# Deferring the lower-half transposed columns of the first image into layer 0, and taking the low part of h from SBUF

## The chip, the cores and the metric

The kernel runs on one core of a Trainium2 chip. The metric is the device time of one execution in microseconds (us). Three runs of the kernel before gave 3059.95, 3065.07 and 3065.65 us; their median is 3065.07 us.

## What is computed

The input `x` has 4 images of 16 channels and 256x256 pixels. Two layers follow each other, each adding to its input a function of the group-normalised input (8 groups of 2 channels):

```
def _L0_conv_ref(x, conv_w, conv_b):                 # K = 5
    out = conv 3x3 of x, 16 -> 16*25 channels, + conv_b
    weights = softmax over the 25 logits of each channel
    return sum over the 5x5 neighbourhood of (x shifted) * weights
...
x = x + _L0_conv_ref(_gn(x), conv_w, conv_b)
x = x + _L1_conv_ref(_gn(x), ...)                    # 3x3, silu and cubic splines
```

The change concerns layer 0 and what prepares its input h = `_gn(x)`. The logits are matrix products that must be nearly exact in fp32: part of the contraction (channel rows of two of the three column shifts and most of the third) is done in fp32, and the rest in the faster fp32r format, for which h is split into a high part `hi` (h rounded to fp32r) and a low part `lo` = h - `hi`.

## The kernel before

**Prologue** (lines 404 to 589). Half-images of `x` (128 rows, 16 channels) are loaded one after the other, and VectorE (`bn_stats`), ScalarE (squares, line 543) and TensorE (line 546) gather the statistics of all four images. While it does this for images 1 to 3, the generator `normalize(0, ...)` is advanced between the statistics (lines 540, 541, 550), so that image 0, which is held in SBUF (`held`), is normalised beside it. The end of the prologue is a flag computed from all images (line 589), on which all engines branch.

**`normalize(b, ...)`** (lines 264 to 401) writes three DRAM scratch tensors of an image: `hs` (h by rows, for the 5x5 sums), and for each half h = 0, 1 of the image `hst[b][h]` (transposed columns of h in fp32) and `hsl[b][h]` (their `hi` and `lo` parts). It works by groups q of 4 channels (4 of them). `rows(q)` makes for each half two ScalarE activations into `hsp` (line 327) and two into `ht` (line 340); `hsp` is stored by `put_rows`. `columns(q, n, h)` (line 349; n = 0, 1) makes four TensorE transposes of `ht` into a PSUM tile `tp`, copies `tp` to the SBUF tiles `tt` (fp32) and `hi` (fp32r), 128x512 elements each, copies one edge column of four elements to the other half, and makes `lo` on VectorE:

```
nc.vector.tensor_sub(
    los[n][:, h, :, 1 : 1 + P], tp, his[n][:, h, :, 1 : 1 + P].bitcast(F32)
)
```

One input of that subtraction, `tp`, is in PSUM and one, `hi`, is in SBUF. After both halves of a pair (q, n), `border` copies the edge columns of `lo`, and `put_columns` issues six DMAs of 260 KB on SP's queue (three for each half). There are 16 steps `columns` to an image. Each is followed by empty steps, so that it takes six steps of the generator; `moves` is a list of actions that fall due some steps later. In the prologue `tt` is copied by VectorE, in layer 0 by ScalarE.

**Layer 0** (`layer0`, lines 620 to 883) runs over 64 strips: 4 images, 2 halves, 8 strips of 32 columns. A strip has 8 groups of 4 columns. For a group, TensorE makes the logits `lg` (three matmuls to a column: two passes of L833 for the fp32 part and one of L837 for the fp32r part), ScalarE takes their exponential into `e` (L856, twice to a group), GpSimd (POOL) multiplies `e` with the 5x5 neighbours `u` (L861, 128x1600 elements, both inputs in SBUF), and VectorE (DVE) sums products and weights (L700, a reduction of 128x3200 elements). There are four `e` tiles. Once to a strip three short VectorE operations divide (L720 to L722; one input of each is the PSUM tile `r`), and POOL subtracts the result from x (L728). The loads of a strip (`am` from `hst`, `an` from `hsl`, `u` from `hs`, `xc` from x) are issued on SP's queue, `am` and `an` two loads ahead.

The preparation of image b+1 runs in layer 0 of image b: after each group, `next(ahead)` (line 870) advances `normalize(b + 1, ...)` by one step. So in layer 0 every operation of `normalize` stands between those of two groups in its engine's queue. The order in the prologue is a scheduler's; in layer 0 `in_order` (line 591) makes it the order in which the code is written.

**Layer 1** (lines 886 to 1110) follows with VectorE, ScalarE and TensorE; POOL has only small operations in it.

Of the kernel before, what the change touches and what calls it, by code (L numbers as in the profile page):

```python
# [3 lines left out]

# [7 lines left out]
F32 = mybir.dt.float32  # L12
F32R = mybir.dt.float32r
AF = mybir.ActivationFunctionType
# [20 lines left out]
def conv_preact_kernel(  # L35
# [12 lines left out]
    nc = tc.nc  # L48
    B, C, H, W = x.shape
    G = 8  # L50
    GC = C // G
    P = 128
    NH = H // P
# [3 lines left out]
    PAD = K // 2  # L57
# [3 lines left out]
    SW = 32  # L61
    NST = W // SW
    SP = SW + 2 * PAD
# [4 lines left out]
    RP = P + 2  # L68
    CT = (W + 2) * RP
    QC = 4  # L70
    QW = W // (P // QC)
    QG = 4
# [8 lines left out]
    const = ctx.enter_context(tc.tile_pool(name="const", bufs=1))  # L81
# [42 lines left out]
    for r in range(RT):  # L124
        p = P // 2 + SROWS.index(r + 1) * C
# [118 lines left out]
    zpad = const.tile([P, QC, PAD], F32, name="zpad")  # L244
    nc.vector.memset(zpad, 0.0)

    def zeros(b, queue):

        for e in (0, HP - PAD):
            for r in range(PAD):  # L250
                yield partial(
                    queue.dma_start,
                    hs[b][:, e + r].rearrange("s c w -> c s w"),
                    zero[0:C, 0 : NST * SP].rearrange("c (s w) -> c s w", s=NST),
                )
        for h in range(NH):
            for w in (0, (W + 1) * RP):
                yield partial(queue.dma_start, hst[b][h][:, w : w + RP], zero[0:C, 0:RP])
                yield partial(
                    queue.dma_start,  # L260
                    hsl[b][h][:, :, w : w + RP].rearrange("c t r -> (c t) r"), zero[:, 0:RP],
                )

    def normalize(b, ptr, tiles, held=None, copier=None):

        prep, xps, tts, his, los = tiles
        copier = copier or nc.scalar.copy

        moves = [(20 + 4 * i, f) for i, f in enumerate(zeros(b, nc.sync))] if held is None else []

        def move():
            for f in [f for i, f in moves if i <= 0]:
                f()
            moves[:] = [(i - 1, f) for i, f in moves if i > 0]

        def load(q, h):
            if held is None and q < C // QC:
                nc.sync.dma_start(  # L280
                    xps[h][:, :, PAD : PAD + W],
                    x[b, q * QC : (q + 1) * QC, h * P : (h + 1) * P, :].rearrange(
                        "c p w -> p c w"),
                )

        def put_rows(q, h, hsp):
            r0 = PAD + h * P
            nc.sync.dma_start(
                hs[b][:, r0 : r0 + P, q * QC : (q + 1) * QC, :].rearrange(
                    "s r c w -> r s (c w)"),  # L290
                hsp.rearrange("p s c w -> p s (c w)"),
            )

        def put_columns(q, n):
            g0 = n * QG
            for h in range(NH):

                for to, ti, t in ((hst, 0, tts[n]), (hsl, 0, his[n]), (hsl, 1, los[n])):
                    d = to[b][h]
                    m = 2 if to is hsl else 1  # L300
                    t = t if t.dtype == F32 else t.bitcast(F32)
                    nc.sync.dma_start(
                        bass.AP(
                            tensor=d.tensor,
                            offset=d.offset + q * QC * m * CT + ti * CT + (1 + g0) * RP,
                            ap=[[QW * RP, W // QW], [m * CT, QC], [1, QG * RP]],
                        ),
                        t[:, h].rearrange("p g r -> p (g r)"),
                    )

        def border(t):
            nc.scalar.copy(t[:, 1, :, 0:1], t[:, 0, :, P : P + 1])
            nc.scalar.copy(t[:, 0, :, RP - 1 :], t[:, 1, :, 1:2])

        hts = {}

        def rows(q):
            for h in range(NH):
                xp = xps[h] if held is None else held[h][:, q * QC : (q + 1) * QC]
                hsp = prep.tile([P, NST, QC, SP], F32, name=f"hsp{b}_{q}_{h}", tag="hsp")  # L320
                ht = prep.tile([P, QW, W // QW, QC], F32, name=f"ht{b}_{q}_{h}", tag=f"ht{h}")
                hts[q, h] = ht
                for k in range(QC // GC):
                    g = q * (QC // GC) + k
                    kc = slice(k * GC, (k + 1) * GC)
                    how = dict(scale=nrm[b][:, 0, g : g + 1], bias=nrm[b][:, 1, g : g + 1])
                    nc.scalar.activation(
                        hsp[:, :, kc, :].rearrange("p s c w -> p c s w"),
                        bass.AP(
                            tensor=xp.tensor, offset=xp.offset + k * GC * (W + 2 * PAD),  # L330
                            ap=[xp.ap[0], [W + 2 * PAD, GC], [SW, NST], [1, SP]],
                        ),
                        AF.Identity, **how,
                    )
                    if k == QC // GC - 1:
                        nc.scalar.copy(hsp[:, 0, :, 0:PAD], zpad)
                        nc.scalar.copy(hsp[:, NST - 1, :, PAD + SW :], zpad)
                        moves.append((4, partial(put_rows, q, h, hsp)))
                    yield
                    nc.scalar.activation(  # L340
                        ht[:, :, :, kc].rearrange("p g w c -> p c w g"),
                        xp[:, kc, PAD : PAD + W].rearrange("p c (w g) -> p c w g", g=QW),
                        AF.Identity, **how,
                    )
                    if k == QC // GC - 1:
                        moves.append((4, partial(load, q + 1, h)))
                    yield

        def columns(q, n, h):

            tp = ptr.tile([P, QG, P], F32, name=f"tp{b}_{q}_{n}_{h}", tag="tp")

            def copy(t, to):

                to(t[:, h, :, 1 : 1 + P], tp)
                if h == 0:
                    to(t[:, 1, :, 0:1], tp[:, :, P - 1 :])
                else:
                    to(t[:, 0, :, RP - 1 :], tp[:, :, 0:1])

            for k in range(QG):
                nc.tensor.transpose(
                    tp[:, k, :], hts[q, h][:, n * QG + k].rearrange("p w c -> p (w c)"), ident
                )
            yield
            copy(tts[n], copier)
            copy(his[n], nc.scalar.copy)
            yield

            nc.vector.tensor_sub(  # L370
                los[n][:, h, :, 1 : 1 + P], tp, his[n][:, h, :, 1 : 1 + P].bitcast(F32)
            )
            if h == NH - 1:
                moves.append((5, partial(border, los[n])))
                moves.append((9, partial(put_columns, q, n)))
            yield
            yield
            yield
            yield

        for h in range(NH):
            load(0, h)
        yield
        for _ in rows(0):
            move()
            yield
        for q in range(C // QC):
            ahead = rows(q + 1) if q + 1 < C // QC else iter(())
            for n in range(QW // QG):
                for h in range(NH):  # L390
                    for k, _ in enumerate(columns(q, n, h)):
                        if k % 3 == 2:
                            next(ahead, None)
                        move()
                        yield
            for _ in ahead:
                move()
                yield
        while moves:
            move()  # L400
            yield


    with tc.tile_pool(name="prep0", bufs=2) as prep, tc.tile_pool(
# [121 lines left out]
        for b in range(B):  # L526
# [44 lines left out]
            if b == 1:  # L571
                prepare1()
            if b == 0:
                ahead = normalize(0, ptr0, tiles, held, nc.vector.tensor_copy)
                next(ahead)
        for _ in ahead:
            pass
# [42 lines left out]
    def layer0(shift):  # L620
# [4 lines left out]
        with tc.tile_pool(name=f"prep{arm}", bufs=2) as prep, tc.tile_pool(  # L625
# [172 lines left out]
            for n, (b, hf, s) in enumerate(strips):  # L798
                if (hf, s) == (0, 0):
                    for _ in ahead:  # L800
                        pass
                    ahead = normalize(b + 1, ptr, tiles) if b + 1 < B else iter(())
                    if b == B - 1:
                        bank = ptr.tile([P, QG, P], F32, name=f"ps{arm}", tag="tp")
                        first_scales = [scales(k, partial(lambda k: bank[:, k], k)) for k in range(2)]
                last = (hf, s) == (NH - 1, NST - 1)
                if last:
                    for _ in ahead:
                        pass
                u = us.pop(0)  # L810
                if s * SW % CX == 0:
# [350 lines left out]
```

## Time and profile before

| | |
|---|---|
| median of 3 runs | 3065.07 us |
| the profiled execution | 3061.86 us |
| its span, first to last instruction | 3059.8 us |
| mean granted TensorE clock | 0.971 |
| busy: TensorE, VectorE, ScalarE, POOL | 92%, 97%, 73%, 64% of the span |
| prologue, to the first layer 0 load | 0 to 120.4 us |
| layer 0, to the last reduction L700 | about 125 to 2047 us |
| layer 1 | about 2047 to 3060 us |

The profile is one execution of the program. A *group* of instructions shares line, engine, operation and tiles: its row has the busy time, the mean of one in ns, and then the idle time of the engine before them with what ended it. The *timeline* lists instructions in order of time with start and duration in us; equal ones that follow each other are merged (x7), and a bracket gives the idle time before and its releaser. A duration can contain a wait inside the instruction. *Busy by stretch* gives the busy time of each engine between two times. PE is TensorE, DVE VectorE, ACT ScalarE, SPq the queue of SyncE, which issues DMAs.

### The profile page before, as it was taken

The numbers are of one execution on the slowest core, as the hardware profiler recorded it, in microseconds if no ns is written. First come the engines' busy times: TensorE is split into PE (matmuls) and PEld (weight loads), VectorE is DVE, ScalarE is ACT, GpSimd is POOL, SyncE is SP. The second block draws the span as 40 slices with busy tenths as digits, with TensorE's granted clock in tenths as the row PEclk, the third lists the DMA queues.
The fourth block names the chain that finished last, engine by engine and source line by source line (L and its number), as shares of the span: only waits on it lengthen the run. The fifth ranks groups of instructions, "written<-read, shape, count | busy, mean of one in ns | idle before, by whom it ended". The sixth has DMA issues, their size and how long they took to land.

```text
span 3059.8 us, 39743 instructions
## 1 busy us (share of the span) xinstructions
PE 2802.6 (92%) x14248; PEld 1448.2 (47%) x14248; DVE 2959.0 (97%) x1587; ACT 2236.6 (73%) x2587; POOL 1947.6 (64%) x744
## 2 busy tenths in 40 slices
PE   4499999999999999999999999958999999999998
PEld 3366656656656666666666566632222222222222
DVE  7599999999999999999999999998999999999997
ACT  6466765676766566766646546559999999999996
POOL 4199999999999999999999999980100100000000
PEclk7699999999999999999999999978999999999999
DMA  8988977879878778978767667659999999999994
GB/s 273 290 223 221 258 205 209 222 189 257 234 209 240 196 202 225 248 216 220 212 174 200 164 173 194 161 131 198 201 192 195 198 194 189 198 194 202 190 197 91
DMA packets 350929, 626.29 MB, mean 205 GB/s; under 512 B 41330, under 2 KB 216676, under 8 KB 334852
## 3 DMA queue, kind: packets, MB, share of 16 engines
q1 hardware_dynamic: 318020, 605.29, 81.0%
q10 hardware_dynamic: 30960, 15.73, 1.8%
q0 software_dynamic: 1744, 2.64, 0.3%
q8 instruction: 117, 1.92, 0.3%
q14 instruction: 88, 0.72, 0.1%
HBM read 513.95 MB, written 104.24 MB: 202 GB/s over the span
## 4 chain that ended last, share of the span: by engine, by line
DVE 69%; issue 11%; PE 8%; DMA 3%; ACT 3%; POOL 2%; SPq 1%; DVEq 0%; ACTq 0%; POOLq 0%
DVE nd L700 44%; PE lg L833 6%; DVE ta L168 4%; DVE ta L167 4%; DVE tb L168 4%; DVE tb L167 4%; DVE tb L158 2%; PE lg L837 1%; DVE yo L1020 1%; POOL e L861 1%; DVE r L721 1%; DVE nd L720 1%; DVE lo L370 1%; DMA am<-hst 1%; DVE nd L722 1%
## 5 line engine op out<-in xcount | busy, mean ns | idle before, releaser
L861 POOL TENSOR_TENSOR e<-e,u 128x1600 f32<-128x1600 f32 x512 | 1788.4, 3539 | 49.0 <-ACT e L856 30.9
L833 PE MATMUL lg<-wm,am 128*128 128x400 f32 x4096 | 1734.8, 505 | 83.8 <-ACT e L856 53.0
L700 DVE TENSOR_REDUCE nd<-e 128x128 f32<-128x3200 f32 x512 | 1748.0, 3478 | 29.0 <-POOL e L861 28.9
L837 PE MATMUL lg<-wn,an 97*128 97x400 f32 x2048 | 1344.9, 657 | 17.3 <-DMA an<-hsl 17.3
L856 ACT ACTIVATE e<-lg 128x800 f32<-128x800 f32 x1024 | 818.2, 837 | 708.9 <-DVE nd L700 460.5
L833 PEld LDWEIGHTS lg<-wm,am 128*128 128x128 f32 x4096 | 760.9, 192 | 403.3 <-ACT e L856 98.2
L1037 PE MATMUL yp<-ring,wt 128*32 128x512 f32 x6144 | 745.9, 598 | 87.6 <-DVE ring L169 63.7
L837 PEld LDWEIGHTS lg<-wn,an 97*128 97x128 f32 x2048 | 388.3, 190 | 334.5 <-issue 23.6
L1037 PEld LDWEIGHTS yp<-ring,wt 128*32 128x32 f32 x6144 | 203.7, 109 | 621.7 <-issue 427.7
L954 POOL MEMSET sl<- 16x256 f32 x6 | 1.8, 306 | 402.7 <-ACT ta L163 299.8
L169 DVE SCALAR_TENSOR_TENSOR ring<-ta,ta 128x2048 f32<-128x2048 f32 (+1 forms) x64 | 147.9, 2310 | 2.5
L168 DVE TENSOR_TENSOR ta<-ta,ta 128x2048 f32<-128x2048 f32 (+1 forms) x64 | 147.5, 2305 | 2.8 <-ACT ta L166 2.8
L169 DVE SCALAR_TENSOR_TENSOR ring<-tb,tb 128x2048 f32<-128x2048 f32 x64 | 145.6, 2275 | 2.5
L748 ACT ACTIVATE z<-xc,nrm 128x256 f32<-128x256 f32 x240 | 144.2, 601 | 5.3 <-POOL xc L728 1.2
L168 DVE TENSOR_TENSOR tb<-tb,tb 128x2048 f32<-128x2048 f32 x64 | 145.4, 2271 | 0.0
L1047 PE MATMUL yp<-sl,ws 64*32 64x512 f32 (+1 forms) x1032 | 131.3, 602 | 0.0
L954 POOL MEMSET slc<- 16x256 f32 x2 | 0.6, 307 | 203.1 <-ACT ta L163 203.0
L166 ACT ACTIVATE ta<-ta 128x2048 f32<-128x2048 f32 (+1 forms) x64 | 123.4, 1928 | 2.0
L193 POOL TENSOR_TENSOR d<-d,nrz 128x8 f32<-128x8 f32 x4 | 2.7, 669 | 191.8 <-DVE d L191 191.8
L166 ACT ACTIVATE tb<-tb 128x2048 f32<-128x2048 f32 x64 | 120.6, 1884 | 0.0
L973 ACT ACTIVATE sl<-sl,q 64x2048 f32<-64x2048 f32 x43 | 90.0, 2094 | 1.1
L728 POOL TENSOR_TENSOR xc<-xc,nd 128x512 f32<-128x512 f32 x64 | 82.5, 1289 | 8.2 <-DVE nd L722 8.2
(195 smaller groups left out, 2089.3 us busy)
## 6 DMA issues: line engine op xcount, KB each, us to landing
am<-hst SPq DMA_DIRECT2D x512, 194.6 KB
u<-hs SPq DMA_DIRECT2D x320, 288.0 KB
an<-hsl SPq DMA_DIRECT2D x512, 129.8 KB
xta<-x1s SPq DMA_DIRECT2D x40, 1024.0 KB
xtb<-x1s SPq DMA_DIRECT2D x40, 1024.0 KB
xtc<-x1s SPq DMA_DIRECT2D x40, 1024.0 KB
am<-hst SPq DMA_DIRECT2D x256, 129.8 KB
sl<-x1s SPq DMA_DIRECT2D x166, 128.0 KB
```

The source lines that it names most:

```text
L166: nc.scalar.activation(s1, r1, AF.Square, scale=2.0)
L167: nc.vector.scalar_tensor_tensor(s2, t, 2.0, s2, ALU.subtract, ALU.mult)
L168: nc.vector.tensor_mul(s1, s1, r1)
L169: nc.vector.scalar_tensor_tensor(f, s2, 0.0, s1, ALU.min, ALU.subtract if given else ALU.add)
L700: nc.vector.tensor_reduce(nd[:, :, :, j : j + JG].rearrange("p t c j -> p t j c"), e.rearrange("p t j m c d -> p t j c m d"), AX.XY, ALU.add,)
L748: nc.scalar.activation(z, v, f, scale=nrm[b][:, 0, g : g + 1], bias=nrm[b][:, 1, g : g + 1], accum_out=st1[b][:, t, g, columns_of(n) : col ...
L833: nc.tensor.matmul(lg[:, i, :NL], lhsT=am[:, o : o + P], rhs=wm.rearrange("p m c d -> p (m c d)"), start=True, stop=False,)
L837: nc.tensor.matmul(lg[:, i, :NL], lhsT=an[:, o : o + P], rhs=wn.rearrange("p m c d -> p (m c d)"), start=False, stop=True,)
L856: nc.scalar.activation(ev, lg[:, :, :NL], AF.Exp)
L861: nc.gpsimd.tensor_tensor(e[:, 1].rearrange("p j m c d -> p j (m c) d"), e[:, 0].rearrange("p j m c d -> p j (m c) d"), uv, ALU.mult,)
L1037: nc.tensor.matmul(yp[t * M : (t + 1) * M], lhsT=wt[:, d, e].rearrange("p r o -> p (r o)"), rhs=ring[:, r0 + t * RT + d : r0 + t * RT + d ...
L1047: nc.tensor.matmul(yp[t * M : (t + 1) * M], lhsT=ws[v, e].rearrange("p r o -> p (r o)"), rhs=sl[n % 3][v, t : t + NT + 1 : NT, e : e + W], ...
```

## The change

1. `normalize` gets a parameter `part`. In the prologue it is called with part 0: for image 0 it still makes `hsp` and `ht` of both halves and all transposes, but only the upper half gets full copies into `tt`, `hi`, `lo` and DMAs to `hst` and `hsl` (three to a pair instead of six). Of the lower half only the edge column that the upper half needs is taken (four elements). The upper half's own last column, which the lower half will need, is kept in three small tiles `kept`.
2. With part 1, `late`, put ahead of `normalize(1)` in the chain that layer 0 of image 0 advances, makes the lower half: it loads x of the lower half again (four loads of 512 KB, into the two `xp` tiles in turn), makes `ht` of that half alone, eight `columns` steps, and three DMAs for each. It is run to its end at the latest in strip 6; the lower half is first needed in strip 8.
3. In layer 0 of image 0, `space=1` leaves one empty step after each `columns` instead of three: four steps instead of six, for `late` and for `normalize(1)`. Images 2 and 3 keep six.
4. Everywhere, `lo` is computed from the copy `tt` in SBUF and no longer from `tp` in PSUM.

```diff
+    NQ = QW // QG
+    kept = [
+        const.tile([P, C // QC * NQ, QG, 1], d, name=f"kept{i}") for i, d in enumerate((F32, F32R, F32R))
+    ]
-    def normalize(b, ptr, tiles, held=None, copier=None):
+    def normalize(b, ptr, tiles, held=None, copier=None, part=None, space=3):
...
+        parts = range(NH) if part is None else (part,)
+        read = range(NH) if part != 1 else (1,)
...
+        def place(q, h):
+
+            return xps[h if part is None else q % 2]
...
         def put_columns(q, n):
             g0 = n * QG
-            for h in range(NH):
+            for h in parts:
...
         def rows(q):
-            for h in range(NH):
-                xp = xps[h] if held is None else held[h][:, q * QC : (q + 1) * QC]
-                hsp = prep.tile([P, NST, QC, SP], F32, name=f"hsp{b}_{q}_{h}", tag="hsp")
+            for h in read:
+                xp = place(q, h) if held is None else held[h][:, q * QC : (q + 1) * QC]
+                if part != 1:
+                    hsp = prep.tile([P, NST, QC, SP], F32, name=f"hsp{b}_{q}_{h}", tag="hsp")
...
-                        moves.append((4, partial(load, q + 1, h)))
+                        moves.append((4, partial(load, q + (1 if part is None else 2), h)))
...
-            def copy(t, to):
-
-                to(t[:, h, :, 1 : 1 + P], tp)
-                if h == 0:
-                    to(t[:, 1, :, 0:1], tp[:, :, P - 1 :])
+            def copy(t, to, keep):
+
+                if h in parts:
+                    to(t[:, h, :, 1 : 1 + P], tp)
+                if part == 1:
+                    to(t[:, 1, :, 0:1], keep[:, q * NQ + n])
+                elif h == 1:
+                    to(t[:, 0, :, RP - 1 :], tp[:, :, 0:1])
                 else:
-                    to(t[:, 0, :, RP - 1 :], tp[:, :, 0:1])
+                    to(t[:, 1, :, 0:1] if part is None else keep[:, q * NQ + n], tp[:, :, P - 1 :])
...
+            v = slice(1, 1 + P) if h in parts else slice(RP - 1, RP)
+            to = h if h in parts else 0
             nc.vector.tensor_sub(
-                los[n][:, h, :, 1 : 1 + P], tp, his[n][:, h, :, 1 : 1 + P].bitcast(F32)
+                los[n][:, to, :, v], tts[n][:, to, :, v],
+                his[n][:, to, :, v].bitcast(F32),
             )
+            if part == 0 and h == 0:
+                moves.append((1, partial(
+                    nc.scalar.copy, kept[2][:, q * NQ + n], los[n][:, 0, :, P : P + 1]
+                )))
+            if part == 1:
+                nc.scalar.copy(los[n][:, 1, :, 0:1], kept[2][:, q * NQ + n])
             if h == NH - 1:
-                moves.append((5, partial(border, los[n])))
-                moves.append((9, partial(put_columns, q, n)))
+                if part is None:
+                    moves.append((5, partial(border, los[n])))
+                moves.append((9 if part is None else 4, partial(put_columns, q, n)))
             yield
+            for _ in range(space):
+                yield
...
-                        if k % 3 == 2:
+                        if (k + 1) % ((3 + space) // 2) == 0:
                             next(ahead, None)
...
-                ahead = normalize(0, ptr0, tiles, held, nc.vector.tensor_copy)
+                ahead = normalize(0, ptr0, tiles, held, nc.vector.tensor_copy, 0)
...
-                    ahead = normalize(b + 1, ptr, tiles) if b + 1 < B else iter(())
+                    ahead = normalize(b + 1, ptr, tiles, space=3 if b else 1) if b + 1 < B else iter(())
+                    if b == 0:
+                        late = normalize(0, ptr, tiles, part=1, space=1)
+                        ahead = chain(late, ahead)
...
+                if n == NST - 2:
+                    for _ in late:
+                        pass
```

More of the change, by code (lines that the diff above doesn't have):

```diff
@@ L2 @@
 from functools import partial
+from itertools import chain
 from itertools import chain
@@ L262, in zeros @@
                 )
-    def normalize(b, ptr, tiles, held=None, copier=None):
+    NQ = QW // QG
[3 more added lines that the diff above has]
+    def normalize(b, ptr, tiles, held=None, copier=None, part=None, space=3):
         prep, xps, tts, his, los = tiles
         copier = copier or nc.scalar.copy
-        moves = [(20 + 4 * i, f) for i, f in enumerate(zeros(b, nc.sync))] if held is None else []
+        moves = [(20 + 4 * i, f) for i, f in enumerate(zeros(b, nc.sync))]
+        moves = moves if held is None and part is None else []
+        parts = range(NH) if part is None else (part,)
+        read = range(NH) if part != 1 else (1,)
         def move():
@@ L280, in load @@
                 nc.sync.dma_start(
-                    xps[h][:, :, PAD : PAD + W],
+                    place(q, h)[:, :, PAD : PAD + W],
                     x[b, q * QC : (q + 1) * QC, h * P : (h + 1) * P, :].rearrange(
@@ L326, in rows @@
                     how = dict(scale=nrm[b][:, 0, g : g + 1], bias=nrm[b][:, 1, g : g + 1])
[L327 to L339, printed above, removed]
+                    if part != 1:
+                        nc.scalar.activation(
+                            hsp[:, :, kc, :].rearrange("p s c w -> p c s w"),
+                            bass.AP(
+                                tensor=xp.tensor, offset=xp.offset + k * GC * (W + 2 * PAD),
+                                ap=[xp.ap[0], [W + 2 * PAD, GC], [SW, NST], [1, SP]],
+                            ),
+                            AF.Identity, **how,
+                        )
+                        if k == QC // GC - 1:
+                            nc.scalar.copy(hsp[:, 0, :, 0:PAD], zpad)
+                            nc.scalar.copy(hsp[:, NST - 1, :, PAD + SW :], zpad)
+                            moves.append((4, partial(put_rows, q, h, hsp)))
+                        yield
                     nc.scalar.activation(
@@ L365, in columns @@
             yield
-            copy(tts[n], copier)
-            copy(his[n], nc.scalar.copy)
+            copy(tts[n], copier, kept[0])
+            copy(his[n], nc.scalar.copy, kept[1])
             yield
+            v = slice(1, 1 + P) if h in parts else slice(RP - 1, RP)
+            to = h if h in parts else 0
             nc.vector.tensor_sub(
-                los[n][:, h, :, 1 : 1 + P], tp, his[n][:, h, :, 1 : 1 + P].bitcast(F32)
-            )
+                los[n][:, to, :, v], tts[n][:, to, :, v],
+                his[n][:, to, :, v].bitcast(F32),
+            )
+            if part == 0 and h == 0:
[4 more added lines that the diff above has]
+                nc.scalar.copy(los[n][:, 1, :, 0:1], kept[2][:, q * NQ + n])
             if h == NH - 1:
-                moves.append((5, partial(border, los[n])))
-                moves.append((9, partial(put_columns, q, n)))
+                if part is None:
+                    moves.append((5, partial(border, los[n])))
+                moves.append((9 if part is None else 4, partial(put_columns, q, n)))
             yield
-            yield
[L378 to L383, printed above, removed]
+            for _ in range(space):
+                yield
+        for h in read:
+            load(0, h)
+            if part == 1:
+                load(1, h)
+        yield
+        if part == 1:
+            yield
         for _ in rows(0):
@@ L389, in normalize @@
             for n in range(QW // QG):
-                for h in range(NH):
+                for h in read:
                     for k, _ in enumerate(columns(q, n, h)):
-                        if k % 3 == 2:
+                        if (k + 1) % ((3 + space) // 2) == 0:
                             next(ahead, None)
```

## The prediction

> **What bounds the kernel now.** I read the busy times by stretch first, then the chain of waits, then the groups of layer 0, and last the timelines. The chain names the bound, and one stretch of 100 us inside layer 0 (columns: PE, PEld, DVE, ACT, POOL busy, clock, DMA share, GB/s) shows how near the next engine is:
>
> ```profile
> DVE 69%; issue 11%; PE 8%; DMA 3%; ACT 3%; POOL 2%; SPq 1%; DVEq 0%; ACTq 0%; POOLq 0%
> ...
> 1500.00:1600.00 100.00, 96.66 (x335) 61.96 (x333) 99.72 (x40) 53.82 (x86) 100.00 (x32) 1.00 0.80 200
> ```
>
> In layer 0 VectorE never waits: eight reductions L700 start 3.394 us apart (27.15 us), the three divisions add 2.04 us, so a strip takes 29.19 us. POOL's strip is as full: its products follow each other at 3.487 us, eight are 27.9, and the subtraction adds 1.24, 29.1 in all. What is added to VectorE's queue lengthens layer 0 one for one. The operation that the change alters everywhere has this row:
>
> ```profile
> L370 DVE TENSOR_TENSOR lo<-tp,hi 128x512 fp32r<-128x512 f32 x48 | 32.7, 681 | 0.0
> ```
>
> 48 of them lie in layer 0, with no wait; the next operation starts 0.60 us after each.
>
> The start of layer 0 is the other place that matters:
>
> ```profile
> 120.44 1.87 SPq L648 DMA_DIRECT2D am<-hst  x3
> ...
> 147.17 0.87 ACT L327 ACTIVATE hsp<-xp,nrm 128x576 f32<-128x576 f32 x1 [11.30 <-DMA am<-hst]
> ...
> 161.04 24.49 DVE L700 TENSOR_REDUCE nd<-e 128x128 f32<-128x3200 f32 x7 [0.53 <-POOL e L861]
> ```
>
> The first load is issued at 120.44, after the last column DMAs of the prologue (to 118.95). ScalarE then stands 11.3 us before an activation of `normalize(1)`, whose x tile was asked for at 137.75 behind the first loads. VectorE runs without a gap only from 161.04, with four reductions behind it: as if it had started at 161.04 - 4 x 3.39 = 147.5.
>
> [...] Before, every VectorE operation of layer 0 above 0.2 us has one input in PSUM or is a reduction of one. The trace has the contention elsewhere. The same two small POOL operations (timeline of POOL), in layer 0 beside reductions and in layer 1 beside two-input operations of VectorE:
>
> ```profile
> 1718.76 1.64 POOL L194 TENSOR_TENSOR p<-d,mhalf 128x8 f32<-128x8 f32 x1
> ...
> 1720.76 0.20 POOL L196 TENSOR_TENSOR p<-p,gsel_sb 128x8 f32<-128x8 f32 x1
> ...
> 2169.84 3.60 POOL L194 TENSOR_TENSOR p<-d,mhalf 128x8 f32<-128x8 f32 x1
> ...
> 2174.25 2.25 POOL L196 TENSOR_TENSOR p<-p,gsel_sb 128x8 f32<-128x8 f32 x1
> ```
>
> ```profile
> 2169.62 2.29 DVE L167 SCALAR_TENSOR_TENSOR ta<-xtb,ta 128x2048 f32<-128x2048 f32 x1
> ...
> 2174.15 2.29 DVE L169 SCALAR_TENSOR_TENSOR ring<-ta,ta 128x2048 f32<-128x2048 f32 x1
> ```
>
> L194 lasts 1.64 us and then 3.60: it ends 1.5 us after L167 does, about its own length. L196 takes 0.20 in layer 0 and here 2.25, to the end of L169. VectorE waits in its turn; this operation on two elements takes 0.21 us otherwise, and here it ends (41.60) with POOL's product (41.58):
>
> ```profile
> 37.33 4.27 DVE L565 TENSOR_SCALAR hm<-hm,ms 128x2 f32<-128x2 f32 x1
> ```
>
> ```profile
> 38.63 2.95 POOL L498 TENSOR_TENSOR sw<-sw,ss 128x1296 f32<-128x1296 f32 x1
> ```
>
> L565 has a single tensor input, so that a two-input VectorE operation waits out a long POOL product is not shown here; a small case is L168 at 2317.11, 2.49 us instead of 2.28, beside a POOL copy that ended at 2317.46. [...]
>
> **The change part by part.**
>
> *Prologue.* It loses 24 of 48 column DMAs: 24 x 260 KB = 6.2 MB, at the 339 to 359 GB/s of the stretches from 80 to 120 us some 18 us of DMA time; 8 x (0.68 + 0.68) - 8 x 0.15 = 9.7 us of VectorE (full `tt` and `lo`, small ones left); 8 x 0.60 + 16 x 0.20 - 8 x 0.20 = 6.4 us of ScalarE (`hi`, borders, kept columns). All three are busy from 40 to 100 us (ScalarE 53 of 60). In the changed order the last columns stand before the flag: the 3.3 us of columns after it (113.3 to 116.5) go, and so does the tail of SP's issues to 118.95; late next is the flag itself, behind the last half-image's statistics. I take the first load 10 us earlier, with 6 (only tail and issues) and 13 as ends.
>
> *First loads.* ScalarE meets its first `ht` one group later and needs one x tile of 512 KB, behind loads that no longer queue behind column writes. Of the 11.3 us I take 8 gone, 3 to 9. Together 18 us, 9 to 22.
>
> *Layer 0 of image 0.* Eight `lo` more: 8 x 0.60 = 4.8 us on VectorE, unhidden. ScalarE gets 8 x 1.32 (`ht`) + 8 x (0.58 + 0.62) + 24 x 0.2 = 25 us in five strips; it sits idle 167 us before L856 between 165 and 640, so nothing. TensorE gets 32 transposes, 0.44 us for four: 3.5 us; a strip of matmuls at 0.857 us a column is 27.4 against VectorE's 30, so nothing, at full clock. SP's queue gets 24 stores and 4 loads, each standing before `am` and `an` loads that run two ahead (four groups, 14.6 us); a store falls due four groups after its `lo`, so it doesn't wait. If that cover were gone, the loads behind would wait for `lo`. POOL's queue gets nothing. The moved 6.2 MB and the 2.1 MB read again spread over 150 us (55 GB/s), in stretches that move 190 to 280 GB/s where 340 is shown, and `normalize(1)` begins that much later: nothing. Four steps instead of six put 24 columns into 15 strips: the same work, denser.
>
> *`lo` from SBUF.* `tp` comes free after ScalarE's copy; nobody waited for it (0.9 us in all of layer 0), so no gain. The cost: each of 8 + 48 = 56 operations now has two SBUF inputs beside POOL's products. VectorE gets to `lo`, finds a product under way, waits for its end; behind it stand the reductions, and behind those the exponentials that wait for `e` tiles and POOL itself. How long? I laid the 48 `lo` of the trace over POOL's timeline. These two rows give boundaries every 3.5 us from 157.49, so at 185.45 nothing is left of a product and at 208.45 it is 1.5 us:
>
> ```profile
> 157.49 52.51 POOL L861 TENSOR_TENSOR e<-e,u 128x1600 f32<-128x1600 f32 x15 [0.49 <-ACT e L856]
> ```
>
> ```profile
> 185.45 0.68 DVE L370 TENSOR_TENSOR lo<-tp,hi 128x512 fp32r<-128x512 f32 x1
> ...
> 208.45 0.68 DVE L370 TENSOR_TENSOR lo<-tp,hi 128x512 fp32r<-128x512 f32 x1
> ```
>
> Over all 48 the rest is between 0.01 and 3.47 us, evenly spread, mean 1.68. As VectorE falls back, POOL has 29.1 us of work in about 30.15 + 1.6 x 1.6 = 32.7 and is in a product 0.89 of the time: 0.89 x 3.487 / 2 = 1.55 us a wait. Bounds: after a wait both start together, and four products (13.95) outlast four reductions (13.58) by 0.37; if every pair falls so, the wait is 0.37. Where the division (2.04) lies between, POOL is already in its fifth product and the wait is 1.8 to 3.4. So 0.37 to 2.6 as a mean; I take 1.55: 56 x 1.55 = 87 us.
>
> **Sum.** Own time of the profiled execution 3061.9 - 18 + 4.8 + 87 = 3136; the median of runs stands 3 us above it: 3139 us.
>
> **The rivals.**
> - *No wait for the port (0.07).* [...] Then 3065 - 18 + 5 = 3052 us, faster. Place: the 56 `lo`; it decides below a mean wait of (18 - 4.8) / 56 = 0.24 us. For it: no row here shows a long product holding off a two-input operation. Against: L194 and L196, stopped to the end of VectorE's instruction.
> - *Waits locked to the boundary (0.04).* Mean 0.37: 56 x 0.37 = 21; 3065 - 13 + 21 = 3073 us, or, with a start gain of 22, 3069. For it: 13.58 against 13.95. Against: the divisions shift VectorE by 2.04 every eight groups.
> - *POOL wins each boundary (0.05).* VectorE waits one product more: 56 x (1.55 + 3.49) = 282; about 3334 us. For it: L565 above was ready at 37.4 and let POOL's issues of that moment pass too. Against: from 2048 to 2055 us POOL's copies and VectorE's two-input operations took turns, one by one.
> - *The prologue doesn't shorten.* The flag waits for loads of x anyway: gain 0 to 9 instead of 18, 3148 to 3157 us; inside the forecast's range.
>
> **How the numbers follow.** The forecast has 0.84. Its own range takes a mean wait of 0.5 to 2.6 us: 3065 - 13 + 28 = 3080 to 3065 - 13 + 146 = 3198, widened to 3200 for the smaller start gain. Only the rivals outside, 0.07 + 0.04 + 0.05, and a rest at its ends lie beyond. A measurement tells about 0.2% (6 us) from no change. Faster 0.08, same 0.03, slower 0.89.
>
> **What would show it.** Right: rows of `lo` in layer 0 with durations between 0.7 and 4 us, mean about 2.2, or the wait as idle time before them; VectorE and POOL alternating there; the strips of images 0 to 2 longer by 2 to 3 us, those of image 3 at 29.19; the first `am` near 110 us; the first ScalarE stall under 5 us. Wrong: `lo` at 0.68 us throughout, or the strips of image 3 longer too.

## The result, and the profile after

The changed kernel takes 3154.83 us (median of 4 runs, 3149.32 to 3159.39) beside 3065.36 us of the kernel before (3059.95 to 3069.93): ratio 1.0292, 95% interval 1.0268 to 1.0315. It is slower by about 90 us, where 3139 (3080 to 3200) was forecast. The profiled execution has a span of 3152.6 us, 92.8 more than before.

The chain of waits by engine, and the stretch of layer 0 that the prediction showed of before, now of the changed kernel (columns: PE, PEld, DVE, ACT, POOL busy, clock, DMA share, GB/s):

```profile
DVE 74%; issue 11%; DMA 5%; PE 4%; ACT 3%; POOL 2%; SPq 1%; DVEq 0%; POOLq 0%; ACTq 0%
...
1500.00:1600.00 100.00, 92.69 (x324) 59.56 (x323) 99.80 (x38) 51.80 (x88) 94.22 (x29) 0.98 0.68 191
```

VectorE is still the bound and still not idle in this stretch: 69% of the chain has become 74%, and its busy share is as before. What fell is the work done in 100 us: 40 instructions of VectorE have become 38, 335 matmuls 324, 32 instructions of POOL 29. VectorE is as busy and gets less done, so the time must be inside its instructions. The groups of layer 0 by form (columns: busy us, mean ns, idle before) say in which. First the reductions before (110 to 2047 us) and after (110 to 2142 us):

```profile
L700 DVE TENSOR_REDUCE nd<-e 128x128 f32<-128x3200 f32 x512 | 1748.0, 3478 | 29.0 <-POOL e L861 28.9
```

```profile
L735 DVE TENSOR_REDUCE nd<-e 128x128 f32<-128x3200 f32 x512 | 1749.0, 3476 | 22.1 <-POOL e L903 22.1
```

Then `lo` after:

```profile
L394 DVE TENSOR_TENSOR lo<-tt,hi 128x512 fp32r<-128x512 f32 x56 | 141.8, 2532 | 0.0
```

The reductions are what they were. `lo` has gone from 681 to 2532 ns and shows no idle time before it: this profile books its wait as duration (one such wait stands below). 56 x (2.532 - 0.681) = 103.6 us.

The start of layer 0 in the timelines of SP, ACT and DVE of the changed kernel:

```profile
109.19 2.93 SPq L683 DMA_DIRECT2D am<-hst  x3
...
134.38 1.29 ACT L359 ACTIVATE ht<-xp,nrm 128x512 f32<-128x512 f32 x1 [4.74 <-DMA am<-hst]
...
125.81 6.97 DVE L735 TENSOR_REDUCE nd<-e 128x128 f32<-128x3200 f32 x2 [13.45 <-POOL e L903]
...
140.68 6.97 DVE L735 TENSOR_REDUCE nd<-e 128x128 f32<-128x3200 f32 x2 [3.90 <-POOL e L903]
```

The first load leaves at 109.19 instead of 120.44 and the first reduction starts at 125.8 instead of 136.9. ScalarE's stall is 4.74 us instead of 11.30, and VectorE still stands idle for 3.90 us after it.

I cut both executions at the first reduction of each image (two of the experiments below stand beside them; us, from the timeline of DVE; layer 1 is the span less the end of the last reduction):

| stage | before | after | lo from PSUM again | before, lo from SBUF |
|---|---|---|---|---|
| to the first reduction | 136.9 | 125.8 | 125.2 | 136.0 |
| image 0 | 485.8 | 528.0 | 488.1 | 520.4 |
| image 1 | 477.3 | 511.0 | 476.7 | 506.0 |
| image 2 | 477.2 | 506.8 | 476.7 | 502.9 |
| image 3, to its last reduction | 470.2 | 470.1 | 470.1 | 470.2 |
| layer 1 | 1012.4 | 1010.9 | 1010.1 | 1011.9 |
| span | 3059.8 | 3152.6 | 3046.8 | 3147.4 |

Images 0 to 2, beside which `lo` is made, take 42, 34 and 30 us longer. Image 3, which has no `lo`, takes the same.

One wait, in the timelines of DVE and POOL of the changed kernel:

```profile
270.78 3.91 DVE L394 TENSOR_TENSOR lo<-tt,hi 128x512 fp32r<-128x512 f32 x1
274.61 3.47 DVE L735 TENSOR_REDUCE nd<-e 128x128 f32<-128x3200 f32 x1
```

```profile
267.13 7.00 POOL L903 TENSOR_TENSOR e<-e,u 128x1600 f32<-128x1600 f32 x2
...
270.61 7.45 POOL L903 TENSOR_TENSOR e<-e,u 128x1600 f32<-128x1600 f32 x2
```

The two POOL lines come from two windows and share a product: it starts at 270.61 and ends at 267.13 + 7.00 = 274.13. `lo` starts 0.17 us into it and ends at 274.69, 0.56 us after it, about its own length. The pair from 270.61 takes 7.45 us instead of 7.00: the next product was already waiting, and the 0.45 us in which `lo` went first are booked on it. Here each engine waits until the other's instruction ends (VectorE 274.13 - 270.78 = 3.35 us, POOL 0.45), and each shows the wait as its own duration.

### The profile page after: what moved, and what is told of

It reads as the page before. It is cut to its first block, busy times and chain, and to the rows that moved or that the text cites. A ratio compares the mean times of both kernels' runs of the same rounds, so it can differ in the third digit from the quotient of the medians.

```text
span 3152.6 us, 39846 instructions
## 1 busy us (share of the span) xinstructions
PE 2834.8 (90%) x14280; PEld 1460.8 (46%) x14280; DVE 3059.3 (97%) x1587; ACT 2248.0 (71%) x2619; POOL 1969.0 (62%) x744
## 4 chain that ended last, share of the span: by engine, by line
DVE 74%; issue 11%; DMA 5%; PE 4%; ACT 3%; POOL 2%; SPq 1%; DVEq 0%; POOLq 0%; ACTq 0%
DVE nd L735 47%; DVE ta L169 4%; DVE lo L394 4%; DVE ta L168 4%; DVE tb L169 4%; DVE tb L168 4%; DVE tb L159 2%; PE lg L875 2%; POOL e L903 2%; DVE yo L1062 1%; DVE r L756 1%; DVE nd L755 1%; DMA xtc<-x1s 1%; DVE nd L757 1%; PE yp L1079 1%
## 5 line engine op out<-in xcount | busy, mean ns | idle before, releaser
L875 PE MATMUL lg<-wm,am 128*128 128x400 f32 x4096 | 1758.0, 510 | 157.6 <-ACT e L898 136.0
L903 POOL TENSOR_TENSOR e<-e,u 128x1600 f32<-128x1600 f32 x512 | 1808.4, 3566 | 136.9 <-ACT e L898 121.3
L394 DVE TENSOR_TENSOR lo<-tt,hi 128x512 fp32r<-128x512 f32 x72 | 148.1, 2064 | 3.1 <-ACT hi L375 3.1
L194 POOL TENSOR_TENSOR d<-d,nrz 128x8 f32<-128x8 f32 x4 | 2.6, 658 | 189.7 <-DVE d L192 189.7
```

What stands on the lines that cost most here:

```text
L394: nc.vector.tensor_sub(los[n][:, to, :, v], tts[n][:, to, :, v], his[n][:, to, :, v].bitcast(F32),)
L875: nc.tensor.matmul(lg[:, i, :NL], lhsT=am[:, o : o + P], rhs=wm.rearrange("p m c d -> p (m c d)"), start=True, stop=False,)
L903: nc.gpsimd.tensor_tensor(e[:, 1].rearrange("p j m c d -> p j (m c) d"), e[:, 0].rearrange("p j m c d -> p j (m c) d"), uv, ALU.mult,)
```

## The experiments

Theory: `lo` with two inputs in SBUF waits for POOL's product. The expectations call it the port theory; the port is the author's assumption, and the traces show only the waits. Rivals: the deferred half or its denser steps cost the time; `lo` is slow by its operands alone. Runs 3 to 6, 8 and 9 are one execution each; they are read by the durations of `lo`, and their spans carry no interval.

**1. `lo` from PSUM again, the rest of the change kept.**

```diff
-                los[n][:, to, :, v], tts[n][:, to, :, v],
+                los[n][:, to, :, v], tp if h in parts else tp[:, :, 0:1],
```

> The changed kernel with one part undone: lo is again made from tp in PSUM, so it has one input in SBUF. Everything else of the change stays (deferred lower half, one step to a group, two tiles of x). Port theory: lo falls from a mean of 2.53 us to 0.68 in layer 0, and the time is that of before less the earlier start (15.8 us) plus 8 more lo at 0.60: about 3054 us, ratio to before 0.9965 (0.994 to 0.999). Rival, the deferral and the denser steps cost the time: lo drops little or the idle of VectorE grows, and the time stays over 3100.

Measured 3051.13 us beside 3061.3, ratio 0.9974 (0.996 to 0.9988). Its row in layer 0:

```profile
L394 DVE TENSOR_TENSOR lo<-tp,hi 128x512 fp32r<-128x512 f32 x56 | 38.1, 680 | 0.0
```

One operand decides: 2532 ns become 680, and the span falls by 105.8 us, the 103.6 of `lo` and 2 more in other places. Deferral and denser steps don't cost the time. They gain 13 us in the span of the profiled execution (see the table) and 10 us in the medians. That is 0.3%, with an interval that stays just below 1.

**2. The kernel before with only `lo` from SBUF.**

```diff
-                los[n][:, h, :, 1 : 1 + P], tp, his[n][:, h, :, 1 : 1 + P].bitcast(F32)
+                los[n][:, h, :, 1 : 1 + P], tts[n][:, h, :, 1 : 1 + P], his[n][:, h, :, 1 : 1 + P].bitcast(F32)
```

> The kernel before with only the one part done: lo from the copy tt in SBUF. All 48 lo of layer 0's images 1 to 3 and the 4 in its last steps, nothing deferred. Port theory: lo 2.3 to 2.6 us as a mean in layer 0, 48 x 1.55 to 1.85 = 74 to 89 us more: 3140 to 3154 us, ratio 1.024 to 1.029. Rival, the wait belongs to the denser steps of the changed kernel: lo under 1 us and the time within 0.3% of before.

Measured 3151.4 us, ratio 1.03 (1.0285 to 1.0316), just above the ratio expected. The 48 `lo` beside POOL's products (137 to 2142 us):

```profile
L370 DVE TENSOR_TENSOR lo<-tt,hi 128x512 fp32r<-128x512 f32 x48 | 122.2, 2547 | 0.0
```

Their mean is 2.547 us, 1.87 more than before: 48 x 1.87 = 89.6 us, and the span grew by 87.6. The wait is as long here, with six steps to a column, as in the changed kernel with four. So it comes from the operand and not from the steps.

**3. POOL writes and reads nothing.**

```diff
-                    nc.gpsimd.tensor_tensor(
-                        e[:, 1].rearrange("p j m c d -> p j (m c) d"),
-                        e[:, 0].rearrange("p j m c d -> p j (m c) d"), uv, ALU.mult,
-                    )
+                    for _ in range(2):
+                        nc.gpsimd.memset(e[:, 1], 1.0)
```

> The changed kernel, with the product on POOL left out and two fills of the same tile put in its place, so that POOL writes but reads nothing; lo has its two inputs in SBUF as in the changed kernel. Port theory (the wait is for POOL's reads): lo 0.68 us mean, below 0.8. Rival, the wait is for anything POOL does: lo over 1.5. Rival, a lo with two inputs in SBUF is slow by itself or beside ScalarE's and the DMAs' accesses: lo stays near 2.5 us. VectorE's reductions stay at 3.4, so that the span is about 3152 less 100 under the port theory.

The rows of `lo` and of POOL's fills in layer 0:

```profile
L394 DVE TENSOR_TENSOR lo<-tt,hi 128x512 fp32r<-128x512 f32 x56 | 38.2, 682 | 0.0
```

```profile
L904 POOL MEMSET e<- 128x1600 f32 x1024 | 1463.7, 1433 | 362.6 <-DVE nd L735 332.7 <-DVE q L200 0.5
```

POOL is busy for 1464 us of layer 0 and `lo` has both inputs in SBUF, yet it takes 0.682 us. Each of the 56 `lo` runs beside a fill for at least 0.54 us of its 0.68. So `lo` isn't slow by its operands, and not beside anything that POOL does: it waits for the product. A fill lacks the product's reads, and also its multiplication; this run alone doesn't part the two. For the reads speaks the prediction's L168, which took 0.2 us longer (2.49 instead of 2.28) beside a POOL copy, a read without a multiplication. The span is 3036.8 us.

**4. POOL's product in two halves.**

```diff
+                    for i in range(0, JG, JG // 2):
...
                         nc.gpsimd.tensor_tensor(
-                            e[:, 1].rearrange("p j m c d -> p j (m c) d"),
-                            e[:, 0].rearrange("p j m c d -> p j (m c) d"), uv, ALU.mult,
+                            e[:, 1, i : i + JG // 2].rearrange("p j m c d -> p j (m c) d"),
+                            e[:, 0, i : i + JG // 2].rearrange("p j m c d -> p j (m c) d"),
+                            uv, ALU.mult,
```

> The changed kernel with POOL's product in two instructions of 128x800 in place of one of 128x1600. Port theory, exclusive for one instruction: the wait ends with a half (about 1.75 us), so the longest lo falls from 4.07 to about 2.4, the mean wait from 1.85 to about 0.9 (lo 1.5 to 1.7 us mean). Rival, POOL holds the port for its whole queue or until both halves are done: lo keeps its 2.5. The span mixes this (56 x 0.9 = 50 us less) with POOL's price for twice as many instructions, and is no test by itself.

The mean missed: 3.07 us instead of 1.5 to 1.7, and the span is 3196.7. Part of that is POOL's price for two instructions: image 3, which has no `lo`, takes 487.8 us instead of 470.1. Of the 56 `lo`, 43 did what the theory said: mean 1.65, longest 2.26. The other 13 took 4.7 to 11.8 us. The longest but two, in the timelines of DVE and POOL of this run:

```profile
165.10 11.58 DVE L394 TENSOR_TENSOR lo<-tt,hi 128x512 fp32r<-128x512 f32 x1
```

```profile
159.79 16.35 POOL L908 TENSOR_TENSOR e<-e,u 128x800 f32<-128x800 f32 x9
181.09 9.11 POOL L908 TENSOR_TENSOR e<-e,u 128x800 f32<-128x800 f32 x5 [4.95 <-ACT e L898]
```

`lo` starts at 165.10 in the middle of nine halves that follow each other without a gap to 176.14, and ends at 176.68. It got no turn at any of the boundaries and ended only when POOL had no work left (4.95 us idle, for exponentials that waited for VectorE). All 13 are of this kind.

I then looked for such cases in the changed kernel. There are four in 56: 4.78, 8.43, 10.38 and 10.38 us. Run 2 has three in 48 (5.27, 7.60 and 8.44 us), so the denser steps aren't what makes them. One of the four:

```profile
740.74 10.38 DVE L394 TENSOR_TENSOR lo<-tt,hi 128x512 fp32r<-128x512 f32 x1
```

```profile
738.87 10.49 POOL L903 TENSOR_TENSOR e<-e,u 128x1600 f32<-128x1600 f32 x3
749.31 1.26 POOL L763 TENSOR_TENSOR xc<-xc,nd 128x512 f32<-128x512 f32 x1
...
756.25 3.53 POOL L903 TENSOR_TENSOR e<-e,u 128x1600 f32<-128x1600 f32 x1 [5.68 <-ACT e L898]
```

The product under way, two more and the subtraction all pass; `lo` ends at 751.12, 0.55 us after POOL's last, and POOL is idle until 756.25. So there are two kinds of wait: to the end of the instruction under way, or until POOL is idle. A `lo` of the second kind has missed its turn.

**5. Every `lo` twice.** The same `tensor_sub` stands a second time behind the first (L394, then L398).

> The changed kernel with every lo made twice, the second right behind the first on VectorE, same operands, same result. Port theory with turns (a product already waiting goes next): the second lo waits for a whole product (3.5 us) whenever POOL has one ready, so the mean over all 112 in layer 0 rises from 2.53 to about 3 us, and the span grows by 56 x 3 = 170 us to about 3320. Rival, VectorE keeps the port while it has work: the second takes 0.6 to 0.7 us, the mean over 112 falls to about 1.6, the span grows by 56 x 0.6 = 34 us to about 3186. Rival, the lo is slow by its own operands: both take 2.5 us, 56 x 2.5 = 140.

The rows of the second and the first, from 110 to 2142 us:

```profile
L398 DVE TENSOR_TENSOR lo<-tt,hi 128x512 fp32r<-128x512 f32 x56 | 183.0, 3268 | 1.9
```

```profile
L394 DVE TENSOR_TENSOR lo<-tt,hi 128x512 fp32r<-128x512 f32 x56 | 137.9, 2462 | 0.0
```

The span grows by 181.6 us to 3334.2, and the mean over all 112 is 2.87. The first takes what it did (2.46 us, after 2.53); the second waits for a whole product (3.90 us in 45 cases, 0.69 in the 11 where POOL had none ready). VectorE doesn't go first twice: the product that waited goes next, and the engines take turns, but for two of the 112 that missed theirs (4.88 and 7.61 us).

**6. Five buffers of `e` instead of four** (and two of `xc` instead of three, for the room). This asked what ends the long waits.

```diff
-        ... name=f"x1{arm}", bufs=3) as x1p
+        ... name=f"x1{arm}", bufs=2) as x1p
-                    e = l0.tile(..., tag="e", bufs=LAG + 3)
+                    e = l0.tile(..., tag="e", bufs=LAG + 4)
```

> The changed kernel with five buffers of e in place of four (and, for the room, two of xc in place of three). In the changed kernel 51 of 56 lo of layer 0 got in when the running product ended, four only when POOL had run out of products (4.8, 8.4, 10.4 and 10.4 us), one behind a product that began with it. Theory, a lo that misses its turn waits until POOL is stopped by the buffers of e: with one buffer more the longest grow by one product, to 11.9 and 13.9 us, and POOL's lead in image 3 grows, while most lo stay below 4.1. Rival, the number of buffers has nothing to do with it: the longest stays at 10.4. The span is no test by itself.

Again four of 56 missed their turn: 8.25, 8.28, 10.71 and 10.72 us. The longest didn't grow to 13.9, so a limit by the buffers of `e` is not what the runs show. The rest waited a little longer (mean 2.27, after 2.07); the span is 3154.1.

**7. `lo` from PSUM, and the deferred half two steps later.**

```diff
         if part == 1:
-            yield
+            for _ in range(3):
+                yield
```

> The kernel with lo from PSUM and the deferred lower half (3046.8 us profiled span), with two more empty steps ahead of the deferred half's first ht. There, ScalarE waited 4.95 us in its first ht, with the exponentials of the fourth group queued behind it, and VectorE idled 4.13 us after it. If that ht waits for its own load of x: both stalls fall below 1 us, and the span goes to about 3043, ratio to before 0.996. Rival, am's loads set the pace of the first strip: VectorE's idle stays at 4 us, and the span at 3047.

The first `ht` in run 1, and then in run 7 (timeline of ACT):

```profile
133.61 1.29 ACT L359 ACTIVATE ht<-xp,nrm 128x512 f32<-128x512 f32 x1 [4.95 <-DMA am<-hst]
```

```profile
136.22 1.33 ACT L359 ACTIVATE ht<-xp,nrm 128x512 f32<-128x512 f32 x1
```

The bracket puts the wait down to a DMA of `am` that landed then, but `ht` reads the x tile `xp`. The cause of the stall is shown: two steps later, `ht` no longer waits, VectorE's idle stretch of 4.13 us shrinks to three of 0.27, 1.11 and 0.40, and the first strip takes 30.2 us instead of 33.0. But the span is 3050.7, where 3043 was expected, and the ratio 0.9987 (0.9978 to 0.9996), no better than run 1. Strip 10 of image 0 (the first is strip 0) took 35.7 us instead of 31.4, by a stall that was shorter in run 1 (timelines of DVE and PE):

```profile
437.59 3.49 DVE L736 TENSOR_REDUCE nd<-e 128x128 f32<-128x3200 f32 x1 [3.02 <-POOL e L904]
442.30 3.49 DVE L736 TENSOR_REDUCE nd<-e 128x128 f32<-128x3200 f32 x1 [1.23 <-POOL e L904]
```

```profile
427.62 1.38 PE L876 MATMUL lg<-wm,am 128*128 128x400 f32 x2 [4.79 <-DMA am<-hst]
```

TensorE waits 4.79 us for a load of `am`, POOL then stands 5.04 us for exponentials, and VectorE for POOL. The next column stores are issued only after that wait, from 428.5. Ahead of `am` (417.6) SP's queue issues five loads of `u` and one of x within 2.7 us; in run 1 the five are spread over 12.2 us, with no load of x behind them. That `am` is late for these loads fits, but isn't tested. Image 0 as a whole takes 487.9 us, after 488.1 in run 1: what the first strip and two later ones gained, strips 10 and 14 gave back. The other 3.9 us of the span lie elsewhere, 2.2 of them in layer 1, which is the same in both kernels.

**8 and 9. POOL always ahead, POOL always behind.** These asked when `lo` misses its turn. In run 8 half of the product is left out and filled in its place; in run 9 a quarter of it is made a second time.

```diff
-                        e[:, 1].rearrange("p j m c d -> p j (m c) d"),
-                        e[:, 0].rearrange("p j m c d -> p j (m c) d"), uv, ALU.mult,
+                        e[:, 1, 0 : JG // 2].rearrange("p j m c d -> p j (m c) d"),
+                        e[:, 0, 0 : JG // 2].rearrange("p j m c d -> p j (m c) d"), ...
+                    nc.gpsimd.memset(e[:, 1, JG // 2 :], 1.0)
```

> The changed kernel with half of POOL's product left out: 128x800 by tensor_tensor, the other half filled. POOL then needs about 1.9 + 0.7 = 2.6 us for a group and is always ahead of VectorE. In the changed kernel 4 of 56 lo in layer 0 missed their turn and waited until POOL was idle, in stretches where POOL had several products ready. If a lo misses its turn only when POOL has ready work queued: none misses it here, POOL is mostly idle when lo comes, the longest lo is under 2.5 us and the mean under 1.0. Rival, missing the turn is chance: some lo still last until POOL's next pause, and the mean stays over 1.2.

```diff
+                    nc.gpsimd.tensor_tensor(
+                        e[:, 1, 0:1].rearrange("p j m c d -> p j (m c) d"),
+                        e[:, 0, 0:1].rearrange("p j m c d -> p j (m c) d"), ...
```

> The changed kernel with a quarter of POOL's product made a second time (128x400, about 1 us more), so that POOL needs about 4.6 us for a group, is behind VectorE and nearly always has ready work queued. If a lo misses its turn when POOL has ready work queued: most of the 56 lo wait until POOL has run out of products, over 7 us each, mean over 5. Rival, lo goes at the end of the running instruction whatever is queued: mean 1.5 to 3 us, none over 4.6. The span is no test: POOL bounds layer 0 at 512 x 4.6 = 2360 us.

The row of `lo` in layer 0 in run 8, and then in run 9:

```profile
L394 DVE TENSOR_TENSOR lo<-tt,hi 128x512 fp32r<-128x512 f32 x56 | 50.0, 893 | 0.0
```

```profile
L394 DVE TENSOR_TENSOR lo<-tt,hi 128x512 fp32r<-128x512 f32 x56 | 68.5, 1222 | 0.0
```

Run 8 (span 3055.5) fits the idea that a turn is missed when POOL has work queued: none is missed, the longest `lo` is 2.33 us. Run 9 (span 3584.4) refutes it: POOL is behind throughout, VectorE waits 490 us for it, and again no turn is missed, the longest is 3.13 us. The mean of 1.22 also lies below what its rival expected. What makes a `lo` miss its turn stays open.

Run 9 also shows what the wait hangs on. POOL is busier than in any other run, yet the wait is short. A reduction begins there when POOL ends a group, and lasts 3.48 us beside a product of 3.53, so that `lo` comes just as the product ends: 29 of the 56 take under 0.75 us. In this run it counts at which moment of a product `lo` comes, and not how busy POOL is.

## Why the prediction was right, and where it was off

- *The bound and the sign: right.* VectorE sets layer 0, and what is added to its queue lengthens it one for one: 103.6 us of `lo` and 8 x 0.60 = 4.8 us for eight more of them, less the earlier start of 15.4 us (below), give 93.0; the span grew by 92.8. That the two agree so closely is in part luck: image by image the sum is off by -0.8, +1.0 and +1.2 us, and layer 1, which the change leaves alone, took 1.5 less.
- *The wait for POOL's product: right.* In the traces of before it had small POOL operations that stopped for VectorE (L194 3.60 us instead of 1.64, L196 2.25 instead of 0.20); that a `lo` with two inputs in SBUF waits out a long product was the author's estimate. Runs 1 and 3 show it from both sides: take one input out of SBUF, or the product away from POOL, and `lo` takes 0.68 us. The sum without a wait (3052 us, the first rival) is what run 1 measures with the wait taken away, 3051. The prediction's L565, a `tensor_scalar` with a single tensor input, took 4.27 us instead of 0.21 and ended with POOL's product; no run here explains that one.
- *`lo` from SBUF, 56 x 1.55 = 87 us: the term that was mis-sized.* It is 56 x 1.85 = 103.6. That `lo` itself takes no longer with both inputs in SBUF was the author's estimate; run 3 shows it, 682 ns. 52 `lo` are of the kind that the sum had, no wait or one to the end of the product under way: their mean is 2.07, 1.39 more than 0.68, together 72.4 us. That 1.39 lies near 1.55 is partly luck, for the waits aren't evenly spread, as the prediction took them: 13 of the 56 `lo` start 0.15 to 0.18 us into a product and wait out nearly all of it, and 10 take 0.67 or 0.68 us. The four that missed their turn add 33.96 - 4 x 0.68 = 31.2 us. The prediction had such a thing as a rival for all boundaries ("POOL wins each boundary") and no mixture: it holds for 4 of 56, and costs one to three POOL instructions more where it does.
- *Prologue, 10 us: right.* The first load left 11.25 us earlier, the first reduction 11.1.
- *First loads, 8 us: too much.* ScalarE's stall shrank by 6.6 us, the first strip from 38.1 to 33.8, by 4.3. Together 15.4 instead of 18, inside the 9 to 22. The rest of the stall isn't the old one: in run 7 it goes when the deferred half starts later. The activation that stood there waited for that half's own x tile, with exponentials queued behind it. The part "ScalarE gets 25 us, so nothing" left that out: it counted busy time and not where the queue stands.
- *Image 0, denser steps at nothing: right within 2.5 us.* In run 1 the image takes 2.2 us more than before; 4.8 for eight `lo`, less 5.1 in the first strip (38.1 to 33.0), would make it 0.3 shorter. That leaves 2.5.
- *What would show it.* Strips of images 0 to 2 longer by 2 to 3 us: 2.6, 2.1 and 1.9 as means. Image 3 unchanged: yes. `lo` between 0.7 and 4 us, mean about 2.2: 42 between 0.78 and 4.07, 10 without a wait and four longer, mean 2.53. First `am` near 110, first ScalarE stall under 5 us: 109.19 and 4.74.

## What to carry to other kernels

Before moving a VectorE operand from PSUM to SBUF, look at what POOL does at that moment: here it read SBUF in long instructions and VectorE was the bound, and a 0.68 us operation cost most often the rest of a POOL instruction of 3.5 us (mean 2.53 us). The profile showed such a wait as a longer instruction with no idle time and no releaser (2532 ns, idle 0.0), so compare one row's mean before and after, and its end with the other engine's boundaries. A change of several parts is to be priced part by part: here one part lost 104 us and hid another that gained about 10.

## What the runs showed of the hardware

- Beside POOL's fills in place of its products, the subtraction with both inputs in SBUF cost the same as with one in PSUM: 682 ns, and 680 in run 1, for 128x512.
- In the changed kernel 42 of 56 `lo` waited for the POOL instruction under way and ended 0.54 to 0.56 us after it. In 4 of 56 cases (3 of 48 in run 2, 13 of 56 with the product in halves) `lo` ended only when POOL went idle, up to 11.8 us. Neither the number of `e` buffers nor POOL's backlog explained which.
- Shorter POOL instructions therefore didn't help: with halves 43 waits shrank to a mean `lo` of 1.65 us, but the mean of all rose from 2.53 to 3.07.
